# Adding up gathered rows on DVE instead of TensorE in three layers of a sparse graph network

## The chip, the cores and the metric

The kernel runs on one core of one Trainium2 chip. The metric is device time in microseconds (us). Engines are named as in the profile: PE is TensorE (PEld its weight loads), DVE is VectorE, ACT is ScalarE, POOL is GpSimd, SP is SyncE. SBUF and PSUM are the core's memories with 128 partitions; the tables that rows are gathered from lie in the chip's DRAM.

## The reference

Four attention layers run over a graph of 4096 nodes with 256 features. Each layer normalises its input, applies a ReLU, computes attention over a node's neighbours, and adds the result to its input `x`:

```python
h = jnp.maximum(_layernorm(x), 0.0); x = x + L0(h, adj)   # 4 heads, softmax of leaky_relu, then elu
h = jnp.maximum(_layernorm(x), 0.0); x = x + L1(h, adj)   # 1 head, h @ W + att @ h
h = jnp.maximum(_layernorm(x), 0.0); x = x + L2(h, adj)   # 4 heads
h = jnp.maximum(_layernorm(x), 0.0); x = x + L3(h, adj)   # 4 heads, scores are q . k
```

In every layer the attention of a node is a softmax over itself and its neighbours, and the output is the sum of the neighbours' rows, each times its weight, head by head. The adjacency matrix is sparse: a node has at most 23 neighbours beside itself in the drawn inputs, most have about eight.

## The kernel before, in words

The kernel works on lists of neighbours. A first part (`lists`, lines up to L492) reads the adjacency matrix, finds each node's neighbours, sorts the nodes by their number, and computes layer 0's table of rows. For layer 0 it also handles the first six neighbours of every node (`EARLY`), so that layer 0 has only the rest to gather.

Then `layers` runs the four layers one after another, in an order of instructions that is written out by hand. The sorted nodes form 32 blocks of 128. All nodes of block b are given the same number of neighbours, `CAPS[b]`, from 23 in block 0 to 3 in block 31; these sum to 277 (layer 0: 93, and nine blocks have none). Blocks are taken in the order 0, 31, 1, 30, ..., so that long and short ones alternate.

For each block and each neighbour slot, POOL issues one indirect DMA (L529) that brings 128 rows from the layer's table to one slot of a ring in SBUF, 18432 fp32 values per partition. A row has 264 values in layers 0 and 2, 288 in layer 1, 512 in layer 3. `fill` issues gathers for blocks up to four ahead of the one at work (`AHEAD`), if their ring slots have been given back. A layer's first gather needs the whole table, which the layer before writes block by block: with an indirect send from POOL (L535) for layer 1 and for the output, with SP's queue for layers 2 and 3.

The work on one block, called a step, is this:

- `scores`: DVE computes the neighbours' scores (L660 to L686), takes the maximum (L692) and subtracts it (L693); ACT takes the exponential (L697) into the weights `p`. In layer 1 `mutual` (L705 to L713) also checks the lists.
- `weigh`: DVE sums the weights and divides (L728 to L734), multiplies the block's own row by its weight (L741), and the gathered rows by theirs, in place in the ring, up to eight at a time (L749). TensorE then adds up the rows: for the own row (L745) and for every gathered row (L753) it multiplies by an identity matrix and accumulates in PSUM. In fp32 each such product shows as two matmul records.
- `settle`: DVE adds the sum to `x` (L780; in layer 0 with the elu, L767 to L778; in layer 3 to the output tile, L772) and takes the statistics of the new `x` (L382, L383), from which ACT and DVE make the normalisation (L386 to L396).
- `second`: ACT normalises (L507), PE transposes (L515), ACT copies (L516), and PE multiplies by the next layer's weights (L522).
- `third`: DVE and ACT finish the next layer's rows (L793 to L820), which are then sent to its table.

In the loop of `layer` these parts of different blocks are interleaved. At step i the block b = i is scored and weighed; block i - 1 has its sum added to `x` and its statistics taken after that; block i - 2 goes through `second` before the weighing and through `third` at the end. The ring slots of b are given back when PE has read them.

Of the kernel before, what the change touches and what calls it, by code (L numbers as in the profile page):

```python
# [9 lines left out]
F32 = mybir.dt.float32  # L10
# [4 lines left out]
ALU = mybir.AluOpType  # L15
AX = mybir.AxisListType
# [3 lines left out]
P = 128  # L20
# [45 lines left out]
class Sparse:  # L66
# [505 lines left out]
    def layer(self, l):  # L572

        nc, nt, vs = self.nc, self.nt, {}
        wide = (W, WL, W, 2 * D)[l]
        slots = RING // wide
        ring = self.ring[:, : slots * wide].rearrange("p (k w) -> p k w", w=wide)  # L580
        todo, held, at = list(ORDER), {}, 0
        made = []

        def fill(i):
            nonlocal at
            while todo and nt - len(todo) <= i + AHEAD:
                j = todo[0]
                K = self.slots(l, j)
                s = (at if at + K <= slots else 0) if K else 0
                if any(s < e and b < s + K for b, e in held.values()) or (l == 3 and len(held) > 3):  # L590
                    return
                todo.pop(0)
                if l == 0:
                    self.fetch(self.rx[j], self.own0, self.own(j))
                if l == 3:
                    vs[j] = self.pool.tile([P, D], F32, name=f"s_vself_{j}", tag="vself", bufs=5)
                    nc.sync.dma_start(out=vs[j], in_=self.tab[3][ts(j, P), D:])
                k0 = EARLY if l == 0 else 0
                for k in range(K):
                    at_k = self.near[:, j, k0 + k : k0 + k + 1]  # L600
                    self.fetch(ring[:, s + k, :], self.tab[l], at_k)
                held[j] = (s, s + K)
                at = s + K if K else at

        acc, behind, rows = {}, {}, {}

        def first(c):
            behind[c] = self.settle(l, c, acc.pop(c), made)
            next(behind[c])

        def second(d):
            if l < 3:
                ht = self.turned(self.pool, next(behind.pop(d)), f"{l + 1}_{d}")
                rows[d] = self.advance(l + 1, d, ht, made)
                next(rows[d])

        def third(d):
            if l < 3:
                next(rows.pop(d), None)
            for send in made:  # L620
                self.send(*send)
            made.clear()

        for i in range(nt):
            fill(i)
            b, c, d = (ORDER[k] if k >= 0 else None for k in (i, i - 1, i - 2))
            if c is not None:
                first(c)
            g = ring[:, held[b][0] : held[b][1], :]
            p = self.scores(l, b, self.rows[b], g)  # L630
            if d is not None:
                second(d)
            acc[b] = self.weigh(l, b, vs.pop(b) if l == 3 else self.rows[b][:, 0:D], g, p)
            del held[b]
            if c is not None:
                next(behind[c])
            if d is not None:
                third(d)
        c, d = ORDER[-1], ORDER[-2]
        first(c)  # L640
        next(behind[c])
        second(d)
        second(c)
        third(d)
        third(c)

    def scores(self, l, b, mine, g):


        nc, pool = self.nc, self.pool  # L650
        H = 1 if l == 1 else 4
        K = self.slots(l, b)
        if K == 0:
            return None
        e = pool.tile([P, TOPK, H], F32, name=f"s_e_{l}_{b}", tag="e", bufs=3)
        ek = e[:, : K + 1, :].rearrange("p k h -> p (k h)")
        if l < 3:
            src = mine[:, D + H : D + 2 * H]
            if l > 0:
                nc.vector.tensor_tensor(e[:, K, :], mine[:, D : D + H], src, ALU.add)  # L660
            nc.vector.tensor_tensor(
                e[:, :K, :], g[:, :, D : D + H], src.unsqueeze(1).to_broadcast([P, K, H]), ALU.add
            )
            if l == 1:
                self.mutual(b, g)

                nc.scalar.copy(self.near[:, b, 0:K], g[:, :, WL - 1])
            slope = 0.01 if l == 1 else 0.2
            el = ek if l > 0 else ek[:, : K * H]
            nc.vector.scalar_tensor_tensor(el, el, slope, el, ALU.mult, ALU.max)  # L670
            if l == 0:
                nc.vector.tensor_copy(e[:, K, :], mine[:, D : D + H])
        else:
            q = self.pe.tile([P, D], F32, name=f"s_q_{b}", tag="q", bufs=1)
            nc.scalar.copy(q, mine[:, 0:D])
            nc.scalar.copy(e[:, K, :], self.eself[:, b, :])
            for k0 in range(0, K, AT_ONCE):
                m = min(AT_ONCE, K - k0)
                kq = g[:, k0 : k0 + m, 0:D]
                nc.vector.tensor_tensor(  # L680
                    kq, kq, q.unsqueeze(1).to_broadcast([P, m, D]), ALU.mult
                )
                nc.vector.tensor_reduce(  # L683
                    e[:, k0 : k0 + m, :], kq.rearrange("p k (h d) -> p k h d", h=4), AX.X, ALU.add
                )
            nc.vector.tensor_tensor(  # L686
                e[:, :K, :], e[:, :K, :],
                self.away[:, b, :K].unsqueeze(2).to_broadcast([P, K, 4]), ALU.add,
            )
        by_head = e[:, : K + 1, :].rearrange("p k h -> p h k")  # L690
        top = pool.tile([P, H], F32, name=f"s_m_{l}_{b}", tag="m", bufs=3)
        nc.vector.tensor_reduce(top, by_head, AX.X, ALU.max)  # L692
        nc.vector.tensor_tensor(  # L693
            by_head, by_head, top.unsqueeze(2).to_broadcast([P, H, K + 1]), ALU.subtract
        )
        p = self.pe.tile([P, TOPK, H], F32, name=f"s_p_{l}_{b}", tag="p", bufs=2)
        nc.scalar.activation(p[:, : K + 1, :].rearrange("p k h -> p (k h)"), ek, AF.Exp)  # L697
        return p

# [15 lines left out]
    def weigh(self, l, b, me, g, p):  # L715

        nc, pool = self.nc, self.pool
        H = 1 if l == 1 else 4
        K = self.slots(l, b)
        tot = pool.tile([P, H], F32, name=f"s_t_{l}_{b}", tag="t", bufs=3)  # L720
        if K == 0:
            nc.vector.reciprocal(tot, self.before[b])
            mine = tot
        else:
            by_head = p[:, : K + 1, :].rearrange("p k h -> p h k")
            if l == 0:
                was = pool.tile([P, H], F32, name=f"s_was_{b}", tag="was", bufs=2)
                nc.vector.tensor_tensor(was, p[:, K, :], self.before[b], ALU.mult)  # L728
                nc.vector.tensor_reduce(tot, by_head[:, :, :K], AX.X, ALU.add)
                nc.vector.tensor_tensor(tot, tot, was, ALU.add)  # L730
            else:
                nc.vector.tensor_reduce(tot, by_head, AX.X, ALU.add)  # L732
            nc.vector.reciprocal(tot, tot)  # L733
            nc.vector.tensor_tensor(  # L734
                by_head, by_head, tot.unsqueeze(2).to_broadcast([P, H, K + 1]), ALU.mult
            )
            mine = p[:, K, :]
        acc = self.pacc.tile([P, IB], F32, tag="acc", name=f"s_acc_{l}_{b}")
        v0 = 0 if l < 3 else D
        mev = pool.tile([P, D], F32, name=f"s_me_{l}_{b}", tag="me", bufs=2)  # L740
        nc.vector.tensor_tensor(  # L741
            mev.rearrange("p (h d) -> p h d", h=H), me.rearrange("p (h d) -> p h d", h=H),
            mine.unsqueeze(2).to_broadcast([P, H, D // H]), ALU.mult,
        )
        nc.tensor.matmul(acc[:, :D], lhsT=self.ident, rhs=mev, start=True, stop=(K == 0))  # L745
        for k0 in range(0, K, AT_ONCE):
            m = min(AT_ONCE, K - k0)
            v = g[:, k0 : k0 + m, v0 : v0 + D].rearrange("p k (h d) -> p k h d", h=H)
            nc.vector.tensor_tensor(  # L749
                v, v, p[:, k0 : k0 + m, :].unsqueeze(3).to_broadcast([P, m, H, D // H]), ALU.mult  # L750
            )
            for k in range(m):
                nc.tensor.matmul(  # L753
                    acc[:, :D], lhsT=self.ident, rhs=g[:, k0 + k, v0 : v0 + D],
                    start=False, stop=(k0 + k == K - 1),
                )
        return acc[:, :D]

    def settle(self, l, b, acc, made):

# [628 lines left out]
```

## Time and profile before

| what | value |
|---|---|
| median of three runs (lowest, highest) | 1940.77 us (1940.31, 1944.88) |
| the profiled execution: time, span | 2277.38 us, 2275.6 us |
| mean granted TensorE clock in it | 0.75 |
| first gather of layers 0, 1, 2, 3 at | 522.5, 813.5, 1282.3, 1784.6 us |
| busy: PE, DVE, ACT, POOL | 1175.5, 1270.9, 444.1, 1212.4 us |
| L753, PE's sums of gathered rows | 1848 records, 510.0 us busy |
| L745, PE's own rows | 256 records, 107.7 us busy |
| L749, DVE's weighting of gathered rows | 169 instructions, 267.1 us busy |
| L529, POOL's gathers to the ring | 924 instructions, 878.0 us busy |

The profile is one execution, and that one took longer than the timed runs. A line of the page's groups gives the source line, the engine, the operation, what it writes and reads, the count, then busy time and the mean of one in ns, then the engine's idle time before these instructions and what ended it. "remote" there is a semaphore update that no recorded instruction is close to. In a timeline, a line gives the start, the duration, the engine, and in brackets the idle time before it with its releaser. A row of busy times by stretch gives, after the stretch and its length, each engine's busy time with its number of instructions, then the granted clock, the share of time in which the DMA engines were busy, and GB/s.

### The profile page before, as it was taken

How to read it: one execution, taken by the hardware profiler on the slowest of the kernel's cores; microseconds unless marked ns; L12 is line 12 of the kernel's file. 1: busy time of each engine (PE TensorE's matmuls, PEld its weight loads, DVE VectorE, ACT ScalarE, POOL GpSimd, SP SyncE). 2: the span in 40 equal slices, each digit the busy share in tenths (PEclk: the TensorE clock that was granted, in tenths of full speed). 3: DMA queues.
4: the chain of work that ended last, by engine and by line, in shares of the span. 5: the costliest groups of instructions: out<-in, count | busy, mean ns of one | idle time of the engine just before them, and what ended most of it. 6: DMA issues, size and time to landing. Idle time of an engine off the chain costs nothing. (4 is left out here: it accounts for less than half of the span.)

```text
span 2275.6 us, 17106 instructions
## 1 busy us (share of the span) xinstructions
PE 1175.5 (52%) x3977; PEld 795.2 (35%) x3999; DVE 1270.9 (56%) x3688; ACT 444.1 (20%) x1320; POOL 1212.4 (53%) x1354
## 2 busy tenths in 40 slices
PE   4767677611466613454566333566668242445354
PEld 2434334301344402333445222344446131334233
DVE  7657787711466711444466313455569465667666
ACT  5754343000233300111111101112123100000000
POOL 1055666556455457566653375655660465666662
PEclk9887889855687855677788756778789665667777
DMA  8988885305233244333432243333331555666662
GB/s 271 297 288 308 300 259 178 88 13 108 75 99 102 76 88 114 93 104 106 111 104 73 57 110 86 102 100 93 109 107 45 145 171 156 182 181 184 179 180 66
DMA packets 128244, 313.24 MB, mean 138 GB/s; under 512 B 31844, under 2 KB 58983, under 8 KB 128136
## 3 DMA queue, kind: packets, MB, share of 16 engines
q0 software_dynamic: 69088, 207.53, 33.3%
q1 hardware_dynamic: 59048, 104.55, 13.6%
q8 instruction: 34, 0.56, 0.1%
q14 instruction: 74, 0.61, 0.1%
HBM read 276.91 MB, written 35.07 MB: 137 GB/s over the span
## 5 line engine op out<-in xcount | busy, mean ns | idle before, releaser
L529 POOL DMA_INDIRECT s_ring<-s_tab,s_near x924 | 878.0, 950 | 599.5 <-issue 239.8
L753 PE MATMUL s_acc<-s_ring,s_ident 128*128 128x256 f32 x1848 | 510.0, 434 | 80.8 <-issue 59.9
L753 PEld LDWEIGHTS s_acc<-s_ring,s_ident 128*128 128x128 f32 x1848 | 409.6, 224 | 179.1 <-issue 73.6
L745 PE MATMUL s_acc<-s_me,s_ident 128*128 128x256 f32 x256 | 107.7, 511 | 410.6 <-issue 135.3
L749 DVE TENSOR_TENSOR s_ring<-s_ring,s_p 128x256 f32<-128x256 f32 (+7 forms) x169 | 267.1, 1605 | 0.0
L529 POOL DMA_INDIRECT s_g<-s_tab,s_listrow x192 | 184.2, 960 | 113.0 <-issue 53.9
L301 DVE MAX8 s_cand<-s_pt 128x8 f32<-128x256 f32 x512 | 188.4, 419 | 81.6 <-remote 40.5
L745 PEld LDWEIGHTS s_acc<-s_me,s_ident 128*128 128x128 f32 x256 | 61.7, 253 | 436.0 <-issue 232.8
L522 PE MATMUL s_ps<-s_we_l,s_ht 128*128 128x264 f32 x256 | 107.5, 560 | 129.7 <-ACT s_ht L516 92.2
L780 DVE TENSOR_TENSOR s_rx<-s_rx,s_acc 128x256 f32<-128x256 f32 x64 | 26.7, 418 | 246.5 <-remote 240.0
L697 ACT ACTIVATE s_p<-s_e 128x32 f32<-128x32 f32 (+13 forms) x119 | 23.1, 194 | 715.1 <-DVE s_e L693 252.5
L293 PE MATMUL s_pt<-s_low,s_mark 128*128 128x512 fp8e4 x256 | 110.2, 430 | 95.9 <-DVE s_cand L301 45.1
L286 ACT ACTIVATE s_low<-s_raw 128x1024 fp8e4<-128x1024 int32 x128 | 134.5, 1051 | 55.0 <-DMA s_raw<-in_adj_dram 45.1
L522 PE MATMUL s_ps_kv<-s_wkv,s_ht 128*128 128x512 f32 x128 | 88.5, 829 | 94.2 <-issue 69.3
L370 PE MATMUL s_ae<-s_g,s_ident 128*128 128x256 f32 x384 | 111.0, 449 | 19.8 <-issue 11.2
L522 PEld LDWEIGHTS s_ps<-s_we_l,s_ht 128*128 128x128 f32 x256 | 59.9, 259 | 156.2 <-ACT s_ht L516 104.3
L299 PE MATMUL s_pt<-s_places,s_stands 128*128 128x512 bf16 x235 | 100.9, 430 | 0.0
L370 PEld LDWEIGHTS s_ae<-s_g,s_ident 128*128 128x128 f32 x384 | 84.5, 226 | 45.2 <-issue 17.0
L680 DVE TENSOR_TENSOR s_ring<-s_ring,s_q 128x2048 f32<-128x2048 f32 (+7 forms) x48 | 81.0, 1687 | 25.5 <-DMA s_ring<-s_tab,s_near 25.2
L515 PE MATMUL s_pht<-s_ident,s_h 128*128 128x128 f32 x128 | 28.9, 310 | 127.9 <-issue 88.1
L386 ACT ACTIVATE s_y<-s_mv,s_eps 128x1 f32<-128x1 f32 x96 | 28.3, 295 | 312.8 <-DVE s_mv L383 130.9
L772 DVE TENSOR_TENSOR s_out<-s_rx,s_acc 128x256 f32<-128x256 f32 x32 | 13.4, 418 | 133.4 <-remote 99.6
(180 smaller groups left out, 1591.3 us busy)
## 6 DMA issues: line engine op xcount, KB each, us to landing
s_raw<-in_adj_dram SPq DMA_DIRECT2D x128, 512.0 KB
s_ring<-s_tab,s_near POOLq DMA_INDIRECT x924
s_tab<-s_kv SPq DMA_DIRECT2D x32, 256.0 KB
s_own<-s_to SPq DMA_DIRECT2D x32, 134.0 KB
s_tab<-s_rows SPq DMA_DIRECT2D x8, 528.0 KB
s_tab<-s_rx SPq DMA_DIRECT2D x32, 132.0 KB
s_xl<-in_x_dram SPq DMA_DIRECT2D x8, 512.0 KB
s_own<-s_xl SPq DMA_DIRECT2D x8, 512.0 KB
```

The lines of the kernel that those rows point to most:

```text
L286: nc.scalar.activation(lo[:, ts(h, quarter)], raw, AF.Copy, saturate=False, accum_out=sums[:, r, h : h + 1],)
L293: nc.tensor.matmul(pt, lhsT=self.mark, rhs=lo[:, ts(g, IB)], start=True, stop=False)
L299: nc.tensor.matmul(pt, lhsT=stands[:, g, :], rhs=places, start=False, stop=True)
L301: nc.vector.max(out=cand[:, g * (IB // CH) + k, :], in_=pt[:, ts(k, CH)])
L370: nc.tensor.matmul(acc[:, :D], lhsT=self.ident, rhs=g[:, k, 0:D], start=False, stop=(k == E - 1))
L515: nc.tensor.transpose(pt[:, ts(c, P)], h[:, ts(c, P)], self.ident)
L522: self.nc.tensor.matmul(ps[:, :width], lhsT=ht[:, c, :], rhs=w[:, c, :], start=(c == 0), stop=(c == KC - 1),)
L529: self.nc.gpsimd.indirect_dma_start(out=out, out_offset=None, in_=table[:, :], in_offset=bass.IndirectOffsetOnAxis(ap=idx, axis=0),)
L680: nc.vector.tensor_tensor(kq, kq, q.unsqueeze(1).to_broadcast([P, m, D]), ALU.mult)
L745: nc.tensor.matmul(acc[:, :D], lhsT=self.ident, rhs=mev, start=True, stop=(K == 0))
L749: nc.vector.tensor_tensor(v, v, p[:, k0 : k0 + m, :].unsqueeze(3).to_broadcast([P, m, H, D // H]), ALU.mult)
L753: nc.tensor.matmul(acc[:, :D], lhsT=self.ident, rhs=g[:, k0 + k, v0 : v0 + D], start=False, stop=(k0 + k == K - 1),)
```

## The change

In layers 0, 1 and 2 the products with the identity matrix go. DVE forms the sum itself, in the same PSUM tile:

- In layers 0 and 2 a block takes one more slot of the ring, where its own weighted row is written; then one `tensor_reduce` adds over the slots, reading the rows across (the rows lie 264 values apart). The nine blocks of layer 0 with nothing to gather write their own row straight to PSUM.
- In layer 1, which has one head, DVE writes the own row times its weight to PSUM, and one `scalar_tensor_tensor` for each gathered row multiplies it by its weight and adds it to the sum in PSUM. The weights `p` move from PSUM to SBUF there.
- Layer 3 keeps TensorE's sum.

The order within a step also changes. In layers 1 and 2 the sum is added to `x` and the statistics are taken in the block's own step (`late` is 0), and `second` works on block i - 1 rather than i - 2. In layers 0 and 3 these stay one step behind. `third` stays with block i - 2, and POOL's queue holds the same instructions in the same order.

```diff
+        more = 1 if l in (0, 2) else 0
...
-                s = (at if at + K <= slots else 0) if K else 0
+                room = K + more if K else 0
+                s = (at if at + room <= slots else 0) if K else 0
...
+        late = 1 if l in (0, 3) else 0
         for i in range(nt):
             fill(i)
             b, c, d = (ORDER[k] if k >= 0 else None for k in (i, i - 1, i - 2))
-            if c is not None:
-                first(c)
             g = ring[:, held[b][0] : held[b][1], :]
-            p = self.scores(l, b, self.rows[b], g)
-            if d is not None:
-                second(d)
-            acc[b] = self.weigh(l, b, vs.pop(b) if l == 3 else self.rows[b][:, 0:D], g, p)
+            p = self.scores(l, b, self.rows[b], g[:, : self.slots(l, b), :])
+            turn = d if late else c
+            if turn is not None:
+                second(turn)
+            acc = self.weigh(l, b, vs.pop(b) if l == 3 else self.rows[b][:, 0:D], g, p)
             del held[b]
-            if c is not None:
-                next(behind[c])
+            behind[b] = self.settle(l, b, acc, made)
+            next(behind[b])
+            sums = c if late else b
+            if sums is not None:
+                next(behind[sums])
             if d is not None:
                 third(d)
...
+        acc = self.pacc.tile([P, IB], F32, tag="acc", name=f"s_acc_{l}_{b}")[:, :D]
+        if l == 1:
+            nc.vector.tensor_scalar(acc, me, p[:, K, :], None, ALU.mult)
+            for k in range(K):
+                nc.vector.scalar_tensor_tensor(
+                    acc, g[:, k, 0:D], p[:, k, :], acc, ALU.mult, ALU.add
+                )
+            return acc
+        if l == 3:
+            mev = pool.tile([P, D], F32, name=f"s_me_{l}_{b}", tag="me", bufs=2)
+        else:
+            mev = g[:, K, 0:D] if K else acc
...
-            for k in range(m):
-                nc.tensor.matmul(
-                    acc[:, :D], lhsT=self.ident, rhs=g[:, k0 + k, v0 : v0 + D],
-                    start=False, stop=(k0 + k == K - 1),
-                )
-        return acc[:, :D]
+            if l == 3:
+                for k in range(m):
+                    nc.tensor.matmul(
+                        acc, lhsT=self.ident, rhs=g[:, k0 + k, v0 : v0 + D],
+                        start=False, stop=(k0 + k == K - 1),
+                    )
+        if l < 3 and K:
+            nc.vector.tensor_reduce(
+                acc, g[:, : K + 1, 0:D].rearrange("p k d -> p d k"), AX.X, ALU.add
+            )
+        return acc
```

More of the change, by code (lines that the diff above doesn't have):

```diff
@@ L588, in fill @@
                 K = self.slots(l, j)
-                s = (at if at + K <= slots else 0) if K else 0
-                if any(s < e and b < s + K for b, e in held.values()) or (l == 3 and len(held) > 3):
+                room = K + more if K else 0
+                s = (at if at + room <= slots else 0) if K else 0
+                if any(s < e and b < s + room for b, e in held.values()) or (
+                    l == 3 and len(held) > 3
+                ):
                     return
@@ L601, in fill @@
                     self.fetch(ring[:, s + k, :], self.tab[l], at_k)
[L602 to L608, printed above, removed]
-            next(behind[c])
+                held[j] = (s, s + room)
+                at = s + room if K else at
+        behind, rows = {}, {}
         def second(d):
@@ L626, in layer @@
             b, c, d = (ORDER[k] if k >= 0 else None for k in (i, i - 1, i - 2))
-            if c is not None:
-                first(c)
             g = ring[:, held[b][0] : held[b][1], :]
-            p = self.scores(l, b, self.rows[b], g)
-            if d is not None:
-                second(d)
-            acc[b] = self.weigh(l, b, vs.pop(b) if l == 3 else self.rows[b][:, 0:D], g, p)
-            del held[b]
-            if c is not None:
-                next(behind[c])
+            p = self.scores(l, b, self.rows[b], g[:, : self.slots(l, b), :])
[3 more added lines that the diff above has]
+            acc = self.weigh(l, b, vs.pop(b) if l == 3 else self.rows[b][:, 0:D], g, p)
+            del held[b]
+            behind[b] = self.settle(l, b, acc, made)
[3 more added lines that the diff above has]
+                next(behind[sums])
             if d is not None:
@@ L639, in layer @@
         c, d = ORDER[-1], ORDER[-2]
-        first(c)
-        next(behind[c])
-        second(d)
+        if late:
+            next(behind[c])
+            second(d)
         second(c)
@@ L695, in scores @@
         )
-        p = self.pe.tile([P, TOPK, H], F32, name=f"s_p_{l}_{b}", tag="p", bufs=2)
+        if l == 1:
+            p = pool.tile([P, TOPK, H], F32, name=f"s_p_{l}_{b}", tag="p", bufs=2)
+        else:
+            p = self.pe.tile([P, TOPK, H], F32, name=f"s_p_{l}_{b}", tag="p", bufs=2)
         nc.scalar.activation(p[:, : K + 1, :].rearrange("p k h -> p (k h)"), ek, AF.Exp)
@@ L737, in weigh @@
             mine = p[:, K, :]
-        acc = self.pacc.tile([P, IB], F32, tag="acc", name=f"s_acc_{l}_{b}")
-        v0 = 0 if l < 3 else D
-        mev = pool.tile([P, D], F32, name=f"s_me_{l}_{b}", tag="me", bufs=2)
+        acc = self.pacc.tile([P, IB], F32, tag="acc", name=f"s_acc_{l}_{b}")[:, :D]
+        if l == 1:
+            nc.vector.tensor_scalar(acc, me, p[:, K, :], None, ALU.mult)
[6 more added lines that the diff above has]
+            mev = pool.tile([P, D], F32, name=f"s_me_{l}_{b}", tag="me", bufs=2)
+        else:
+            mev = g[:, K, 0:D] if K else acc
         nc.vector.tensor_tensor(
@@ L744, in weigh @@
         )
-        nc.tensor.matmul(acc[:, :D], lhsT=self.ident, rhs=mev, start=True, stop=(K == 0))
+        if l == 3:
+            nc.tensor.matmul(acc, lhsT=self.ident, rhs=mev, start=True, stop=False)
+        v0 = 0 if l < 3 else D
         for k0 in range(0, K, AT_ONCE):
@@ L751, in weigh @@
             )
-            for k in range(m):
-                nc.tensor.matmul(
-                    acc[:, :D], lhsT=self.ident, rhs=g[:, k0 + k, v0 : v0 + D],
-                    start=False, stop=(k0 + k == K - 1),
-                )
-        return acc[:, :D]
+            if l == 3:
+                for k in range(m):
[8 more added lines that the diff above has]
+        return acc
     def settle(self, l, b, acc, made):
```

## The prediction

> **What bounds the kernel now.** I read the page's first part, then busy time in five stretches that I cut at the first gather of each layer (522.4, 813.4, 1282.3 and 1784.6 us), then waits and the timeline inside a stretch. The page's row of engines, and that of the gathers:
>
> ```profile
> PE 1175.5 (52%) x3977; PEld 795.2 (35%) x3999; DVE 1270.9 (56%) x3688; ACT 444.1 (20%) x1320; POOL 1212.4 (53%) x1354
> ...
> L529 POOL DMA_INDIRECT s_ring<-s_tab,s_near x924 | 878.0, 950 | 599.5 <-issue 239.8 <-PE s_acc L753 103.9 <-remote 81.2
> ```
>
> The stretches of layers 0, 1 and 2:
>
> ```profile
> core 0: us, PE busy (x) PEld busy (x) DVE busy (x) ACT busy (x) POOL busy (x), PEclk, DMA share, GB/s
> ...
> 522.40:813.40 291.00, 145.59 (x442) 100.52 (x442) 154.53 (x617) 80.86 (x279) 151.71 (x157) 0.73 0.34 89
> 813.40:1282.30 468.90, 228.45 (x810) 173.25 (x810) 219.80 (x755) 58.13 (x192) 262.71 (x277) 0.73 0.37 97
> 1282.30:1784.60 502.30, 277.92 (x941) 188.68 (x941) 257.33 (x752) 85.91 (x290) 263.13 (x277) 0.77 0.35 92
> ```
>
> No engine is full. What fills the gaps shows in layer 1's timeline:
>
> ```profile
> 1016.26 5.45 PE L753 MATMUL s_acc<-s_ring,s_ident 128*128 128x256 f32 x24
> ...
> 1021.81 0.44 PE L515 MATMUL s_pht<-s_ident,s_h 128*128 128x128 f32 x2
> ...
> 1025.13 0.95 POOL L529 DMA_INDIRECT s_ring<-s_tab,s_near  x1 [0.30 <-issue]
> 1026.39 0.95 POOL L529 DMA_INDIRECT s_ring<-s_tab,s_near  x1 [0.30 <-issue]
> ...
> 1033.90 0.42 DVE L780 TENSOR_TENSOR s_rx<-s_rx,s_acc 128x256 f32<-128x256 f32 x1 [10.22 <-remote]
> ...
> 1035.34 0.37 ACT L516 COPY s_ht<-s_pht 128x256 f32<-128x256 f32 x1 [13.58 <-remote]
> ```
>
> POOL issues one gather each 0.95 + 0.30 = 1.25 us, back to back. DVE's L780 needs the sum that PE's 24 passes make; PE's records end at 1021.7, DVE is released at 1033.9. ACT's copy of the transposes of 1021.8 comes 13 us after them. So PE's completions arrive late after a long burst. Over the run:
>
> ```profile
> DVE s_rx L780 <- remote: 240.0, 21, 68.5
> ...
> DVE s_out L772 <- remote: 99.6, 6, 31.9
> ```
>
> **Profiled time against the median.** The profiled execution took 2277.4 us (2275.6 of span, 1.8 around it), the runs 1940.8: 336.6 less. These two waits sum to 339.6. I therefore test whether the timed runs lack them, with POOL's rate as floor. Layer 0 issues 93 ring gathers, 32 of own rows, 32 sends: 157 x 1.255 = 197; layer 1 277 + 32 sends: 388; layer 2 277: 348. Each layer ends with a tail that POOL can't cover, since the next layer's gathers need the whole table: I estimate 25 us (one gather 1, its landing 3 as in the chain's "DMA s_ring", a DVE step 279/32 = 9, the settling, transposes and products 7, the table's write 5). So 222, 413 and 373 us, where the profile has 291, 469 and 502. With the 522.4 before and the 1.8 outside, 409 of 1940.8 remain for layer 3, whose own floor is 309 x 1.255 + 25 = 413. The floors fill the timed run: I take it that it runs at POOL's rate, and that PE's lateness belongs mostly to the profiled execution. If the first stretch is up to 60 us shorter when timed (it has "remote" waits too), up to 70 of the 321 us by which the four layers exceed their floors, 22%, could be real.
>
> **What the Trainium skill says.** "VectorE: DVE Perf Modes", section on the perf-mode tiers: tensor_reduce, and tensor_tensor on fp32, have only the one-element-a-cycle rate. The trace agrees for dense reads: 2280 and 2286 ns for 2048 elements, about 1.04 ns each. "SBUF — State Buffer", the specifications: a 16-byte line needs at least two hits for full bandwidth, and each new line costs. The new reduction of layers 0 and 2 steps 264 x 4 = 1056 bytes between the rows it adds, one hit a line. Two present reductions step through SBUF too: L439 by 128 bytes, L692 (four heads) by 16. The forms:
>
> ```profile
> L749 DVE TENSOR_TENSOR s_ring<-s_ring,s_p 128x2048 f32<-128x2048 f32 x63 | 143.3, 2280 | 0.0
> L683 DVE TENSOR_REDUCE s_e<-s_ring 128x32 f32<-128x2048 f32 x20 | 45.7, 2286 | 0.7
> ...
> L778 DVE SCALAR_TENSOR_TENSOR s_rx<-s_acc,s_ex 128x256 f32<-128x256 f32 x32 | 13.6, 424 | 1.1
> ...
> L439 DVE TENSOR_REDUCE s_posf<-s_where 128x32 f32<-128x800 f32 x1 | 1.5, 1489 | 0.0
> ...
> L692 DVE TENSOR_REDUCE s_m<-s_e 128x4 f32<-128x8 f32 x4 | 0.6, 162 | 0.1
> ...
> L692 DVE TENSOR_REDUCE s_m<-s_e 128x4 f32<-128x96 f32 x2 | 0.6, 322 | 0.1
> ```
>
> Dense L683: 2286 - 2048 x 1.04 = 158 ns fixed. L439: (1489 - 158) / 800 = 1.66 ns an element. L692: (322 - 162) / 88 = 1.82. I take 1.7, and keep 1.04 as the low end.
>
> **The change, part by part.**
> - Removed in layers 0 to 2: 647 + 96 identity products of two passes (L753, L745). PE isn't the floor above, so this is worth nothing in the timed run, and 254 us if PE's lateness were all real (below).
> - Layers 0 and 2, added: one reduction a block. Layer 2: (277 + 32) x 256 = 79,104 elements x 1.7 = 134.5, plus 32 x 0.158 = 5, together 140 us (87 at 1.04). Layer 0: 23 blocks with gathers, (93 + 23) x 256 = 29,696 x 1.7 + 3.6 = 54 (34.5 at 1.04). The block's own weighted row (L741) only changes its place, at the same 0.42 us.
> - Layer 1: dense multiply (L749) of 79.6 and L741 of 13.5 go; 277 scalar_tensor_tensor on 256 elements come, each waiting for the one before it. L777 and L778 stand such a pair in the trace: 422 and 424 ns, start to start 0.46 (586.31, 586.77). 277 x 0.46 + 32 x 0.45 = 142, net +49. The trace has no DVE sum that stays in PSUM; L778 reads PSUM at 424 against L777's 422 without, so I take no surcharge.
> - Moved: in layers 1 and 2 settling and statistics come in the block's own step, the normalisation, transposes and products one step earlier; the sends and table writes stay where they were in POOL's and SP's order, with the same instructions. DVE no longer meets a PE wait there. At the layer's end one block's transposes and products leave the tail; layer 1's last sum also is shorter (8 x 0.46 against 2.3 plus up to 16 passes of 0.22 to 0.43): I take -5 us for layer 1, and count layer 2's within its tail below.
> - The extra ring slot a block of layers 0 and 2: 62 of 69 slots for the first five blocks. Ring slots come free after DVE's reduction. While DVE is behind, POOL has work four blocks ahead, so no new stall; with DVE ahead, none either.
>
> DVE's load, with gaps under 0.6 us counted as its own (they sum to 20, 20 and 22 us in the three stretches): layer 0 154.5 + 20 + 54 = 228; layer 1 220 + 20 + 49 = 289; layer 2 257 + 22 + 140 = 419. Before a layer's first step DVE waits for the first block's gathers: 27, 34 and 34 us from first issue to first DVE instruction (522.5 to 549.7, 813.5 to 847.5, 1282.4 to 1316.1). So layer 0 takes 27 + 228 + 3 = 258 against POOL's 222: **+36**. Layer 1: 34 + 289 = 323, under 413: hidden by the gathers, **-5**; the cover is 90 us. Layer 2: 34 + 419 + 5 = 458 against 373: **+85**. Layer 3 is as before. Sum +116: 2057 us. If 22% of the lateness is real, the before is that much slower than its floors (22% of 72 + 56 + 129 = 257, thus 57) and the change saves it: 2000. I take the middle, **2028 us**, likeliest's range 1985 to 2070.
>
> In the profiled execution the same sums say shorter, not longer: 291 to 258, 469 to 408, 502 to 458, that is 138 us less, about 2140 of span. The two metrics should part.
>
> **Rivals.**
> 1. Dense rate for the reduction. For it: same opcode and element count as L683. Against: L439 and L692. Layer 2 405, layer 0 239: +32 + 17 - 5 = +44, 1985, or 1957 with the 22%. Slower still.
> 2. Faster: PE's lateness is there in timed runs, at L780. The change is worth 116 - 254f, f being the share that is real; it decides from f = 0.46. At f = 0.7: 1880. For it: the waits are 340 us of recorded time. Against: the sum of floors leaves room for f of 0.22 at most, unless POOL issues faster than 1.25 us when not profiled.
> 3. The long step costs more than the two short ones measured: at 2.5 ns an element 63 us more in layer 2 and 24 in layer 0, 2115. Nothing in the trace shows it.
> 4. DVE hides it all: only if POOL's gathers took over 420 us in layer 2; 1936 to 1941.
>
> **How the numbers follow.** Likeliest 0.60, rival 1 0.14, rival 2 0.14, rival 3 0.08, rival 4 0.04. A measurement here can't tell less than 0.3%, some 6 us, from no change. Slower by more: 0.60 + 0.14 + 0.08, less 0.02 for rival 1 where yet more of the lateness is real, = 0.80; same 0.04; faster 0.14 + 0.02 = 0.16. The range 1935 to 2090 leaves out rival 2 and most of rival 3.
>
> **What would show it.** Right: layer 2's stretch near 458 with DVE over 85% busy and POOL waiting for DVE's reduction; the reduction's mean near 0.16 + 1.7 x 2.47 = 4.4 us; layer 1 still at one gather each 1.25 us; layer 1's accumulating rows at 0.42; no "remote" waits in layers 0 to 2. Wrong: a mean of 2.7 us (dense), DVE waiting for gathers through layer 2, or a median under 1940, which would make PE's lateness real.

## The result, and the profile after

The changed kernel takes 2041.57 us (2040.70 to 2044.71, 4 runs) where the kernel before takes 1940.54 us (1938.60 to 1944.88, 4 runs): ratio 1.052, 95% interval 1.0499 to 1.0541. It is 101 us slower.

To read the comparison, a profile of the kernel before was needed that takes as long as the timed runs; the one shown in the first part took 2277 us. Experiment e9 gave one: the same kernel, span 1931.0 us. It stands for "before" from here on. Beside the experiments e1 to e8 the kernel before itself takes 2272 to 2285 us, beside the comparison above and e9 to e12 it takes 1938 to 1941, so times of whole kernels are read from the latter alone.

The page of the changed kernel, its engines and its gathers:

```profile
PE 894.7 (44%) x2491; PEld 508.4 (25%) x2513; DVE 1527.5 (75%) x3972; ACT 449.6 (22%) x1320; POOL 1209.2 (59%) x1354
...
L529 POOL DMA_INDIRECT s_ring<-s_tab,s_near x924 | 875.8, 948 | 427.2 <-issue 190.3
```

DVE, already the fullest engine before (1272.5 us or 66% in e9), is fuller still, and POOL, with the same gathers at the same 948 ns, is idle longer. Busy times of the changed kernel, in four stretches cut at the first gather of each layer:

```profile
510.80:784.10 273.30, 89.82 (x192) 46.83 (x192) 204.83 (x640) 83.84 (x279) 150.50 (x157) 0.50 0.35 95
784.10:1149.70 365.60, 90.07 (x192) 46.66 (x192) 282.54 (x984) 60.02 (x192) 262.15 (x278) 0.50 0.46 124
1149.70:1608.90 459.20, 198.22 (x320) 81.66 (x321) 401.65 (x784) 86.47 (x290) 263.32 (x277) 0.58 0.37 101
1608.90:2038.90 430.00, 203.75 (x621) 149.90 (x621) 302.39 (x406) 19.54 (x94) 294.15 (x309) 0.71 0.64 188
```

The same of the kernel before, from e9:

```profile
510.00:757.70 247.70, 136.37 (x442) 94.85 (x442) 154.38 (x617) 80.84 (x279) 152.29 (x158) 0.77 0.39 105
757.70:1126.90 369.20, 221.72 (x810) 170.54 (x810) 220.80 (x755) 59.04 (x192) 261.90 (x278) 0.79 0.46 123
1126.90:1501.70 374.80, 265.16 (x941) 183.15 (x941) 258.37 (x753) 86.50 (x290) 263.89 (x278) 0.86 0.46 124
1501.70:1931.00 429.30, 199.46 (x618) 146.39 (x618) 302.57 (x406) 19.55 (x94) 294.28 (x309) 0.71 0.64 189
```

By layer the change is +25.6, -3.6, +84.4 and +0.7 us, together 107; the execution of e9 that is profiled here is 8 us faster than the median of 1940.54, which is why this is more than 101. DVE's busy time (the third number after the length) grows by 50.5, 61.7 and 143.3 us. So layer 1 swallows all of what DVE gained there, layer 2 some 59 us of it, and layer 0 half.

Where it is swallowed is in the waits. DVE's waits in layer 2 of the kernel before (e9; columns: us in total, times, longest):

```profile
DVE s_e L677 <- DMA s_ring<-s_tab,s_near: 65.8, 15, 36.0
DVE s_kv L843 <- PE s_ps_kv L524: 16.6, 18, 3.0
DVE s_rx L816 <- PE s_acc L785: 8.3, 3, 5.3
DVE s_rx L846 <- PE s_ps_q L524: 5.6, 18, 1.0
```

and of the changed kernel:

```profile
DVE s_e L666 <- DMA s_ring<-s_tab,s_near: 36.2, 1, 36.2
DVE s_kv L831 <- PE s_ps_kv L522: 3.5, 1, 3.5
...
```

(Lines of e9 lie lower than in the first part: its L816 is L780 there, its L785 is L753, its L677 is L661.) In the kernel before, DVE waited once for the layer's first gathers and 14 times more for later ones, 30 us, and 30 us for PE. In the changed kernel only the first wait and one of 3.5 us are left (the rest is below 0.7 us each): these lines sum to 96 us before and 40 after, so some 57 us of waits are gone, and 143 of new work less 57 is near the 84 that the layer grew by. From its first gathers on DVE never waits for them, so DVE sets layer 2. POOL waits for it there, also by record, at the reduction that gives ring slots back:

```profile
POOL s_ring L529 <- DVE s_acc L778: 21.7, 8, 5.5
```

The new instructions, by their forms:

```profile
L750 DVE SCALAR_TENSOR_TENSOR s_acc<-s_ring,s_p,s_acc 128x256 f32<-128x256 f32 x277 | 135.7, 490 | 9.7
...
L778 DVE TENSOR_REDUCE s_acc<-s_ring 128x256 f32<-128x2560 f32 x5 | 23.6, 4728 | 0.2
...
L748 DVE TENSOR_SCALAR s_acc<-s_rx,s_p 128x256 f32<-128x256 f32 x32 | 15.6, 486 | 1.1
...
L778 DVE TENSOR_REDUCE s_acc<-s_ring 128x256 f32<-128x1024 f32 x6 | 11.4, 1893 | 0.2
...
L778 DVE TENSOR_REDUCE s_acc<-s_ring 128x256 f32<-128x768 f32 x4 | 4.2, 1040 | 0.1
...
L778 DVE TENSOR_REDUCE s_acc<-s_ring 128x256 f32<-128x512 f32 x4 | 2.8, 703 | 0.1
```

L748 is layer 1's own row times its weight. Ten rows cost 4728 ns for 2560 elements, 1.79 ns an element with the 158 ns fixed taken off. In layer 1's timeline of the changed kernel a step is short and POOL runs on:

```profile
940.59 0.95 POOL L529 DMA_INDIRECT s_ring<-s_tab,s_near  x1 [0.30 <-issue]
...
941.58 0.17 DVE L666 TENSOR_TENSOR s_e<-s_ring,s_rx 128x11 f32<-128x11 f32 x1 [2.22 <-DMA s_ring<-s_tab,s_near]
...
941.84 0.95 POOL L529 DMA_INDIRECT s_ring<-s_tab,s_near  x1 [0.30 <-DMA s_ring<-s_tab,s_near]
...
945.16 3.11 DVE L750 SCALAR_TENSOR_TENSOR s_acc<-s_ring,s_p,s_acc 128x256 f32<-128x256 f32 x6
```

One gather each 1.25 us, and DVE waits 2.22 us for one: there the gathers still set the pace.

What TensorE still has to do became slower. Its products for the next layer's rows in layers 0 and 1 are the same 256 in both kernels. First e9, then the changed kernel:

```profile
L524 PE MATMUL s_ps<-s_we_l,s_ht 128*128 128x264 f32 x256 | 103.1, 540 | 29.6 <-ACT s_ht L518 29.6
```

```profile
L522 PE MATMUL s_ps<-s_we_l,s_ht 128*128 128x264 f32 x256 | 136.1, 685 | 29.5 <-ACT s_ht L516 29.5
```

In the stretches above, where PE's busy time falls, its granted clock falls too: from 0.77 to 0.50 in layer 0, from 0.79 to 0.50 in layer 1, from 0.86 to 0.58 in layer 2. In layer 0 DVE waits 21.0 us for these products where it waited 14.6; in layers 1 and 2 a single longer wait for TensorE is left, 3.7 and 3.5 us.

### The profile page after: what moved, and what is told of

Same layout as the page of the kernel before. It is cut to its first block, busy times and chain, and to the rows that moved or that the text cites. A ratio compares the mean times of both kernels' runs of the same rounds, so it can differ in the third digit from the quotient of the medians.

```text
span 2038.9 us, 14096 instructions
## 1 busy us (share of the span) xinstructions
PE 894.7 (44%) x2491; PEld 508.4 (25%) x2513; DVE 1527.5 (75%) x3972; ACT 449.6 (22%) x1320; POOL 1209.2 (59%) x1354
## 5 line engine op out<-in xcount | busy, mean ns | idle before, releaser
L778 DVE TENSOR_REDUCE s_acc<-s_ring 128x256 f32<-128x1792 f32 (+15 forms) x55 | 198.9, 3616 | 1.9
L768 DVE TENSOR_TENSOR s_ring<-s_ring,s_p 128x2048 f32<-128x2048 f32 (+7 forms) x121 | 187.4, 1571 | 0.0
L773 PE MATMUL s_acc<-s_ring,s_ident 128*128 128x256 f32 x554 | 174.4, 485 | 28.3 <-DVE s_ring L768 28.3
L773 PEld LDWEIGHTS s_acc<-s_ring,s_ident 128*128 128x128 f32 x554 | 136.2, 251 | 71.2 <-DVE s_ring L768 45.1
L522 PE MATMUL s_ps<-s_we_l,s_ht 128*128 128x264 f32 x256 | 136.1, 685 | 29.5 <-ACT s_ht L516 29.5
L750 DVE SCALAR_TENSOR_TENSOR s_acc<-s_ring,s_p,s_acc 128x256 f32<-128x256 f32 x277 | 135.7, 490 | 9.7
L522 PE MATMUL s_ps_kv<-s_wkv,s_ht 128*128 128x512 f32 x128 | 114.9, 1048 | 14.8 <-ACT s_ht L516 14.8
L522 PE MATMUL s_ps_q<-s_w_q,s_ht 128*128 128x256 f32 x128 | 61.9, 634 | 132.2 <-DVE s_kv L831 132.2
L515 PE MATMUL s_pht<-s_ident,s_rx 128*128 128x128 f32 x64 | 22.0, 447 | 217.4 <-ACT s_rx L507 115.5
L763 PE MATMUL s_acc<-s_me,s_ident 128*128 128x256 f32 x64 | 30.7, 572 | 189.0 <-DVE s_me L758 189.0
```

What stands on the lines that cost most here:

```text
L515: nc.tensor.transpose(pt[:, ts(c, P)], h[:, ts(c, P)], self.ident)
L522: self.nc.tensor.matmul(ps[:, :width], lhsT=ht[:, c, :], rhs=w[:, c, :], start=(c == 0), stop=(c == KC - 1),)
L750: nc.vector.scalar_tensor_tensor(acc, g[:, k, 0:D], p[:, k, :], acc, ALU.mult, ALU.add)
L768: nc.vector.tensor_tensor(v, v, p[:, k0 : k0 + m, :].unsqueeze(3).to_broadcast([P, m, H, D // H]), ALU.mult)
L773: nc.tensor.matmul(acc, lhsT=self.ident, rhs=g[:, k0 + k, v0 : v0 + D], start=False, stop=(k0 + k == K - 1),)
L778: nc.vector.tensor_reduce(acc, g[:, : K + 1, 0:D].rearrange("p k d -> p d k"), AX.X, ALU.add)
```

## The experiments

The kernels come from the changed one with a tuple that names the layers in which DVE sums (and in which the new order within the step holds); the empty tuple gives the instructions of before, all three layers those of the change.

**One layer at a time: e1, e2, e3, and e5, e6 again.**

```diff
-DVE_SUM = (0, 1, 2)
+DVE_SUM = (0,)      # e1
+DVE_SUM = (1,)      # e2, e5
+DVE_SUM = (2,)      # e3, e6
```

> Only layer 0 sums on DVE; layers 1 and 2 sum on TensorE in the order of before. Theory A (layer 0 is bound by DVE after the change, by POOL's gathers before): the changed kernel's layer 0 took 273 us against a floor of 222, so 1975 to 1990. Rival B (TensorE's late completions are on the path of timed runs too): layer 0 had few of them, 1930 to 1950.

> Only layer 1 sums on DVE, with the new order within its step. Theory A: layer 1 was at POOL's rate and stays there, hidden: 1925 to 1941. Rival B: layer 1 loses the waits of L780, 100 us of the profiled 469, so 1840 to 1890.

> Only layer 2 sums on DVE, with the new order within its step. Theory A: 459 us where the floor was 373, so 2005 to 2026. Rival B: the profile had 502 us there, 459 after, so 1900 to 1940.

> Only layer 1 sums on DVE, with the new order within its step, as in the second experiment, whose executions lost half of their semaphore records. Theory A (DVE's added work in layers 0 and 2 is the whole loss; layer 1 stays at POOL's rate): the changed kernel's layer 1 took 366 us, its floor is 277 x 1.255 + 25 = 373; so the same as before or a little faster, 1915 to 1941. Rival C (the new order of a step costs by itself): over 1950.

> Only layer 2 sums on DVE, with the new order within its step. Theory A: layer 2 takes 459 us where before took 373 to 395: 2005 to 2027, two thirds or more of the whole loss of 101. Rival C (the loss is spread evenly over the layers, by the order of the step or the clock of TensorE): about a third, 1970 to 1980.

Measured, against 2278.70 us of the kernel before for e1 to e3 and 2271.88 for e5 and e6: e1 2272.19 us, ratio 0.9973 (0.9948 to 0.9998); e2 2297.77, 1.0091 (1.0066 to 1.0117); e3 2289.88, 1.0055 (1.0023 to 1.0087); e5 2283.32, 1.0035 (1.0014 to 1.0056); e6 2287.93, 1.0071 (1.0049 to 1.0093). As tests of where the 101 us come from they are inconclusive: layer 2's stretch was 518 us in e3 against 459 in the changed kernel of the comparison, with the same DVE work, 401.5 us. What lies between shows as waits whose end no recorded instruction explains, and not only waits for PE's sums. These traces also hold fewer records: e3's has 12,667 semaphore updates, e9's 31,291. So behind "remote" there may be a late completion, or one whose record is missing. The longest such waits of e3:

```profile
DVE s_rx L816 <- remote: 142.3, 11, 61.2
ACT s_ht L518 <- remote: 125.9, 12, 16.7
DVE s_out L808 <- remote: 84.3, 7, 19.2
ACT s_to L375 <- remote: 53.2, 7, 8.6
POOL s_ring L531 <- remote: 51.1, 46, 4.9
```

ACT and POOL have them too, also where no sum of PE is waited for: L518 copies transposes. What is safe in these runs is what an engine did: DVE's busy time by layer in e3, 154.3, 220.9, 401.5 and 302.3 us, is that of before in layers 0, 1 and 3 and that of the change in layer 2.

**Half of PE's sums: e4.** The kernel before, with every second gathered row left out of the sums of layers 0 to 2.

```diff
-                for k in range(m):
+                last = K - 1 if l == 3 else (K - 1) // 2 * 2
+                for k in range(0, m, 1 if l == 3 else 2):
                     nc.tensor.matmul(
                         acc, lhsT=self.ident, rhs=g[:, k0 + k, v0 : v0 + D],
-                        start=False, stop=(k0 + k == K - 1),
+                        start=False, stop=(k0 + k == last),
                     )
```

> The kernel before, with every second gathered row left out of TensorE's sum in layers 0 to 2 (DVE still weights all of them; the result is not the reference's). Theory A: timed runs do not wait for TensorE, 1925 to 1941, and the profile's remote waits of L780 fall below 60 us with the profiled execution under 2130. Rival B: timed runs fall by half of what TensorE costs, to 1830 to 1880.

Measured: 2232.59 us against 2278.70, ratio 0.9793 (0.9730 to 0.9856). Halving the bursts of layers 0 to 2 takes 46 us of the some 340 us by which these runs exceed 1940. DVE's "remote" waits at the settling (L817 there) are 96.0 us and not below 60, the profiled execution took 2238 and not less than 2130. So the length of PE's bursts matters a little in these runs, and most of the 340 us has another cause (e7 below is as slow without any of these sums). What that is stays open.

**The sum by dense additions: e7; layers 0 and 1 alone: e8.** In e7 the strided reduction becomes additions of the upper half of the rows to the lower half, until two are left.

```diff
-            nc.vector.tensor_reduce(
-                acc, g[:, : K + 1, 0:D].rearrange("p k d -> p d k"), AX.X, ALU.add
-            )
+            n = K + 1
+            while n > 2:
+                m = n // 2
+                nc.vector.tensor_tensor(
+                    g[:, :m, 0:D], g[:, :m, 0:D], g[:, n - m : n, 0:D], ALU.add
+                )
+                n -= m
+            nc.vector.tensor_tensor(acc, g[:, 0, 0:D], g[:, 1, 0:D], ALU.add)
```

```diff
-DVE_SUM = (0, 1, 2)
+DVE_SUM = (0, 1)    # e8
```

> The changed kernel with its strided reduction in layers 0 and 2 replaced by halving adds over whole rows (tensor_tensor, dense, in place in the ring): layer 2 then has 277 x 256 elements at 1.04 ns and some 4 instructions a block, about 100 us of DVE where the reduction took 146; layer 0 about 36 where it took 52. Theory A (DVE bounds both layers): layer 2 falls from 459 to about 412, the whole by 50 to 65 against the changed kernel, so 1975 to 1992 where before has 1940. Rival C (the reduction is not what bounds, the order of the step is): no fall, 2030 to 2045. If completions come late in this run as in the six before it, only the durations and DVE's sums are to be read: 95 to 105 us for the adds of layer 2.

> Layers 0 and 1 sum on DVE, layer 2 on TensorE as before. Theory A (layer 2 has most of the loss): 1940 to 1970 where before has 1940. Rival C (the loss is spread evenly): about 2005. If completions come late in this run too, 2270 to 2310, and nothing is told apart by its time.

Measured, against 2284.47 us: e7 2303.62, ratio 1.0091 (1.0050 to 1.0133); e8 2297.14, 1.0062 (1.0040 to 1.0083). Again the totals don't tell, but e7 has none of PE's sums in layers 0 to 2 and still takes 2304 us, where it was expected at 1975 to 1992 beside a kernel before of 1940. The durations do tell. The additions in e7, L793 among the rows and L797 the last one into PSUM:

```profile
L793 DVE TENSOR_TENSOR s_ring<-s_ring 128x512 f32<-128x512 f32 (+8 forms) x115 | 102.2, 889 | 10.4 <-DVE s_ring L780 3.1 <-remote 2.2 <-DVE s_ring L793 1.3
...
L797 DVE TENSOR_TENSOR s_acc<-s_ring 128x256 f32<-128x256 f32 x55 | 23.8, 433 | 5.0 <-DVE s_ring L793 2.2 <-issue 1.0
```

126.0 us do what 198.9 us of strided reductions did, with three times the instructions. DVE's busy time in layer 2 falls from 401.7 us in the changed kernel to 347.6. Reading the rows across, and not the number of additions, is thus 73 us of the price. That this is the stride itself is argued and not shown, since e7 changes the instruction too; for it speaks that the same instruction on dense rows (L688) takes 1.04 ns an element. My estimate from that is a layer 2 of 459 - 54 = 405 us, still 30 above the 375 of before; this was not measured where the kernel before takes 1940.

**The kernel before and the changed one, each with its trace: e9, e10.** Both kernels are unchanged.

> The kernel before, unchanged, for a trace of its own beside the runs that follow. Theory (PE's late completions are no part of the 1940 us): if this run takes about 1940, its stretches are near POOL's rate, layer 0 220 to 240, layer 1 365 to 380, layer 2 365 to 385, layer 3 400 to 430, and no 'remote' wait stands above 40 us. If it takes about 2275, as the profile shown of before, the stretches are near 291, 469, 502 and 491 again. Rival (the lateness is part of the 1940 too): a run of about 1940 still shows DVE's waits for PE's sums of over 100 us.

> The changed kernel, unchanged. Theory: if the kernel before takes about 1940 here, this takes 2041, with stretches of 273, 366, 459 and 430 us. If the kernel before takes about 2275, this is within 2% of it (the parts alone gave -6, +19 and +11 us there, their sum +24: 2299), since the waits that the change removes are longer there. Rival (the change costs the same 101 us in both conditions): 2376.

Measured: e9 1937.67 us, ratio to before 0.9995 (0.9978 to 1.0011); e10 2040.79, 1.0517 (1.0480 to 1.0554), with stretches of 273.4, 365.4, 458.9 and 429.8 us. In e9 no wait is put down to "remote" on any engine, and DVE's wait for PE's sum in layer 2 is the 8.3 us shown above (8.1 in layer 1), where the profile of the first part had 240.0 at this line. Layers 1 to 3 of e9 lie where the theory put them. Layer 0 does not, 247.7 us instead of 220 to 240. DVE's waits there tell why:

```profile
DVE s_e L677 <- DMA s_ring<-s_tab,s_near: 27.5, 2, 27.3
DVE s_ex L813 <- ACT s_ex L804: 24.1, 8, 8.4
DVE s_rx L829 <- PE s_ps L524: 14.6, 11, 3.4
DVE s_was L747 <- ACT s_p L716: 7.7, 8, 1.6
```

In layer 0 DVE is held, in the kernel before, by the elu, whose exponential on ACT needs PE's sum of the step before, and by the products of the next layer's rows. In the changed kernel the wait at the elu is 0.4 us.

**Layer 1 alone, once more: e11.**

```diff
-DVE_SUM = (0, 1, 2)
+DVE_SUM = (1,)
```

> Only layer 1 on DVE. Theory (layer 1 stays at POOL's rate, its sum is hidden): if the kernel before takes about 1940 here, this takes 1930 to 1945, with layer 1's stretch at 365 us. If about 2275, again some 10 to 20 us above the kernel before (1.0035 and 1.009 so far). Rival (layer 1 has a part of the 101 us): 1960 or more where before takes 1940.

Measured: 1936.60 us against 1938.49, ratio 0.9987 (0.9974 to 1.0000). Layer 1 pays nothing, as the theory said, and what it gains can't be told from nothing either. Its stretch, and DVE's wait for gathers in it:

```profile
762.10:1127.40 365.30, 90.09 (x192) 46.70 (x192) 282.37 (x984) 60.02 (x192) 262.09 (x278) 0.50 0.47 124
```

```profile
DVE s_e L677 <- DMA s_ring<-s_tab,s_near: 51.3, 11, 37.7
```

The kernel before waits 116.4 us at this place (e9). The 61.7 us of added work came out of that wait; 51.3 - 37.7 = 13.6 us are left behind the first gathers. So the cover was nearly used up.

**The reductions left out: e12.** The changed kernel, with a copy of the own row in the reduction's place.

```diff
-            nc.vector.tensor_reduce(
-                acc, g[:, : K + 1, 0:D].rearrange("p k d -> p d k"), AX.X, ALU.add
-            )
+            nc.vector.tensor_copy(acc, g[:, K, 0:D])
```

> The changed kernel with the reductions of layers 0 and 2 left out: a copy of the block's own weighted row takes their place, so the gathered rows aren't summed there. DVE loses 199 us of reductions and gains 55 copies of some 0.4 us, 22 us. Theory (the reductions set layers 0 and 2, and POOL's rate is the next bound): layer 2's stretch falls from 459 to about 373, layer 0's from 273 to about 230, so 2041 becomes about 1910 where before takes 1940; where before takes 2275, it falls by 60 to 130 against the changed kernel. Rival (the order of settling and statistics, not the reduction, costs the time): less than 30 us below the changed kernel.

Measured: 1905.95 us, 134.8 below e10; ratio to the kernel before 0.9818 (0.9784 to 0.9852). Layers 0 and 2:

```profile
511.70:742.80 231.10, 89.86 (x192) 47.00 (x192) 160.86 (x640) 83.85 (x279) 151.25 (x157) 0.51 0.41 113
...
1108.00:1476.30 368.30, 175.30 (x323) 73.73 (x323) 269.12 (x785) 86.47 (x290) 263.68 (x277) 0.66 0.47 126
```

Layer 2 falls by 90.6 us to 368.3, though DVE's work falls by 132.4: from there on the gathers set the pace (277 x 1.255 = 348, and 20 us of tail), and DVE waits for them again, 16 times and 73.5 us. Layer 0 falls by 42.3 us for 43.9 us of work. With the order of the change, and with neither PE's sums nor the reductions, the kernel is 33 us faster than before. So the reductions cost more than the whole difference, and the order together with PE's missing sums costs nothing; e12 doesn't part these two. That is the rival's end: it asked for less than 30 us below the changed kernel.

Of the versions that compute the whole none is clearly faster than the kernel before: the interval of e11 ends at 1.0000, that of e1, beside which the kernel before takes 2279 us, at 0.9998.

## Why the prediction was right

The direction, the mechanism and the size were right: 2028 forecast, 2041.57 measured. The sum without any lateness gave 2057, and that is the right one to compare, since e9 shows that the share f of PE's lateness in the timed runs is nil. Taking the middle between 2057 and 2000 moved the forecast from 15 us above the measurement to 14 below it; that this did no harm was luck. Step by step:

- **PE's lateness is not in the timed runs.** Right. The sum of POOL's floors against the timed run was the argument, and e9 shows it. That it was *PE's* lateness was wrong: e3 has such waits on ACT and POOL as well, halving PE's sums (e4) takes only 46 us away, and e7 is slow without them. The step held because it asked only whether the timed runs had room for it. The 22% was also a wrong sum. With 60 us less in the first stretch, 1477 us are left for floors of 1421; that is 56 of the 332 us by which the four layers of the profile exceed them, 17%, and would have made the forecast 2036. (The 72 in the sum of 257 should be 291 - 222 = 69, which moves nothing.) In e9 the first stretch is 12 us shorter, 510.0.
- **The floors.** They summed to 222 + 413 + 373 + 413 = 1421 us, and e9's four layers take 1421.0 us. The parts were off by -26, +44, -2 and -16. The +44 is a mistake of mine: the 32 sends of layer 1's table are issued in layer 0, where I counted them, and I counted them a second time in layer 1. Layer 0's -26 goes with the chain through the elu and the products, which I had not looked for (46 us of DVE's waits in e9); layer 3's -16, the same in e9 to e12, was not followed up. The errors cancelled by luck, and a total that fits did not show it.
- **Layer 2, +85.** Right: +84.4 and 459 against 458. DVE's busy time was forecast at 257 + 140 = 397 and is 401.7; the first wait at 34 and is 36.2; what is left, 27 against 21.
- **The reduction.** Right: 146.3 us in layer 2 against 140 and 52.6 in layer 0 against 54, mean 4571 ns against 4400. The dense 1.04 ns is a slope: L688 takes 2286 ns for 2048 elements and 686 for 512. The rate of 1.7 ns an element, read from two short instructions with a stride, is 1.69 at four rows and 1.77 to 1.79 above. That agrees with the Trainium skill, "SBUF — State Buffer", specifications, which has a penalty for each crossing to a new 16-byte line without a number for DVE; it does not agree at two and three rows, where the same stride costs 1.06 and 1.15 ns.
- **Layer 0, +36.** The sign was right, the size is +25.6. Its end was forecast at 258 and is 273.3: the term for waits on PE was 3 us, and DVE waits 21.0 us for the product L522 there. The forecast had no term for these products running slower once PE does less; the wait for them was 14.6 us in e9. The start was forecast at 222 and is 247.7. The failing step is the floor of POOL's rate in layer 0, taken without reading its waits.
- **Layer 1, -5.** Right in size (-3.6 here, -3.9 in e11), with too large a cover: I gave 90 us, of which 40 are the sends counted twice, and 13.6 were left. The added work was 61.7 us where I had 49: an accumulating instruction takes 490 ns and starts each 0.518 us (3.11 us for six), where I took 0.46.
- **"No surcharge" for a sum that stays in PSUM.** The instruction takes 490 ns where I took 424, but staying in PSUM is not what costs the 66 ns. L748 writes to the same tile, accumulates nothing, reads no PSUM, and takes 486 ns; e7's additions that end in PSUM (L797) take 433. What L748 and L750 share is a factor read from `p`, one value for each partition, where L777 and L778 have constants. No run parts that from the rest, so the cause stays open. The Trainium skill, "VectorE: DVE Perf Modes", section on the perf-mode tiers, gives tensor_tensor with an operand in PSUM the same one-element rate that it has on fp32 in SBUF. The trace of e7 agrees: 433 ns for L797 against 426 for the same addition in SBUF (L793 on 256 elements).
- **Rivals.** The dense rate: no, 4571 ns is not 2.7 us. PE's lateness real: no, by e9. A costlier stride: no. DVE hides it all: true of layer 1 alone.
- **The two metrics part.** I said that in conditions like those of the profile shown, the change would shorten the span by 138 us. The changed kernel as a whole was not run there, so this is untested; but its parts alone gave -6, +19 and +11 us (e1 to e3), and e7, with all three layers on DVE and a cheaper sum than that of the change, +19, which speaks against it. Taking PE's sums away does not take the "remote" waits away.

## What to carry to other kernels

Before a profile is priced, compare its own time with the timed runs; if they differ by a sixth, find the floor that the timed run must obey, and price against that, layer by layer with each layer's own instruction list, since a total that fits can hide two errors. An engine that is idle at half the span is no free place for work: what it can take is what it waits in that stage, here 79 us for gathers in layer 1 (116.4 less the first 37.7) and 57 for gathers and PE in layer 2, and a sum of 62 us fits where one of 143 doesn't. A sum across the rows of the ring cost DVE 198.9 us; additions row by row took a third less, 126.0. Work taken from TensorE can also slow what it keeps: here the same products went from 540 to 685 ns.

## What was not expected of the hardware

- The strided reduction over two or three rows (512 and 768 elements, 703 and 1040 ns) runs at 1.06 and 1.15 ns an element, near the dense 686 and 952 of L688; over four rows it jumps to 1893 ns, 1.69 an element. Why the step lies between three and four rows was not tried.
- The small reductions over four heads, with 16 bytes between the values, cost less where they read PSUM. The maximum over `e` in SBUF (L697) takes 202 ns for 28 elements and 243 for 52, 1.71 ns for each further one; the sum over `p` in PSUM (L740) takes 183 and 209, 1.08. The operations differ, so the memory as the cause is not shown.
- An accumulation of 256 elements in place in PSUM takes 490 ns and a product without accumulation (L748) 486, both with one factor for each partition; the accumulating operation with constants takes 416 to 424.
- TensorE's granted clock differs between the layers of one execution: in e11 it is 0.77 in layer 0 and 0.86 in layer 2, where PE forms the sums, and 0.50 in layer 1, where it does not.
- In the profile of the first part and in e1 to e8, waits of up to 69.5 us (e1) end without a recorded cause, on DVE, ACT and POOL alike; in the changed kernel's profile and in e9 to e12 none do. The first kind of trace holds 11,916 to 13,516 semaphore updates, the second 30,757 to 31,291. Whether completions come late there or are only not recorded, and why these runs take longer, stays open. The experiments lay on four chips (e1 to e4, e5 and e6, e7 and e8, e9 to e12), so the chip is not excluded.
